# The division of a softmax moved from TensorE transposes to DMA, in six of eight batches

## Chip, cores and metric

One core of a Trainium2 chip runs the whole program. The metric is the device time of one execution in microseconds; the lower, the better.

## What is computed

A transformer block of four parts over x of shape (8, 512, 256), each with a layer norm before it and the input added after it: attention A, a feed-forward net, a retention-like attention B, and the same feed-forward net again. The change lies in attention A alone. Cut to what matters:

```python
att = einsum('bhqd,bhkd->bhqk', q, k) / sqrt(HEAD_DIM)      # 16 heads of 16
att = att + (log_sparse + log(decay + 1e-09))               # depends on distance only
att = softmax(att, axis=-1)
out = einsum('bhqk,bhkd->bhqd', att, v)
out = out + 0.2 * sigmoid(q . mean(k)) * mean(v)
return out.reshape(B, T, 256) @ Wo + bo
```

Softmax needs one division for each row and head. The kernel multiplies the unnormalised probabilities by v first and divides the 16 values of a head by the row's sum afterwards.

## The kernel before

**Tiles and loops.** Batches b (8) times groups g (4 heads each) give 32 items i = 4b + g. An item has eight score steps. In a step TensorE makes a 128x1024 tile of scores `s` for two heads, VectorE takes its row maxima (`mr`), and, ten steps later, TensorE makes the transposed scores `t` of another pair of heads with the maximum already subtracted. ScalarE takes the exponential (`p`), and VectorE or GpSimd multiplies by the table of distances `dec_a`. `pv_item` (line 539) multiplies by v: the tile `pv` is 128x512, 32 rows for each of the four heads, of which 16 are values, one is the row's sum (v carries a column of ones) and the others are unused. All 512 queries stand side by side.

**The division.** `post_units(i)` (line 555) makes up to three units. `evacuate`: ScalarE copies `pv` from PSUM to `num`. `divide`: TensorE turns `num` with four 128x128 transposes, so that queries lie on partitions; VectorE takes the reciprocals of the sums (`rd`, 128x16) and multiplies them into `a_tok`. `turn`, after each second group: TensorE turns half of `a_tok` back with four transposes, and ScalarE copies them into `aT`, where the 128 rows of a half are 8 heads of 16 values. `wo_unit` (line 599) multiplies `aT` by Wo.

**Order.** All engines' instructions are pinned to the order in which the program writes them. That order is planned: a loop at the end keeps an estimated clock for each engine, and work is a chain of `Unit`s (line 292) with a cost on TensorE (`pe`), costs on other engines after it (`then`), predecessors (`after`), things that it gives or needs (`gives`, `needs`), and banks of PSUM. `start_of` (766) says when a unit may start, `issue` (778) writes it and moves the clocks. The loop writes score steps and, between them, units of the other chains: the next batch's projections (`front1`, `front2`), the rest of earlier batches (`rest`: Wo, both feed-forward nets, attention B), and `posts`, the chain of `post_units`, which is looked at first. A unit without TensorE's cost is written as soon as its start is no more than 300 ns ahead of TensorE's planned clock. `turn` of `front2` writes the next batch's `kT` and `qT` by way of DRAM; for keys its step is 32(b - 1) + 14, where the batch's first score is step 32b.

**Queues.** All transfers but the shift of the maxima (`shift`, line 492, on ScalarE's queue) go through `move` (line 90) on SP's queue, in program order. Small PSUM tiles (`misc`, line 210) share three banks. In the profile line 69 is the helper for VectorE, ScalarE and GpSimd, 205 a matmul, 208 a transpose, 91 a transfer of SP.

Of the kernel before, what the change touches and what calls it, by code (L numbers as in the profile page):

```python
# [9 lines left out]
F32 = mybir.dt.float32  # L10
# [5 lines left out]
P = 128  # L16
B, T, D = 8, 512, 256
NH, HD = 16, 16
HH = 8
NG = 4  # L20
NT = T // P
NC = D // P
# [13 lines left out]
def tile_kernel(  # L36
# [37 lines left out]
    dve, act, gps = Engine(nc.vector), Engine(nc.scalar), Engine(nc.gpsimd)  # L74
# [4 lines left out]
    at = ctx.enter_context(tc.tile_pool(name="at", bufs=2))  # L79
    rs = ctx.enter_context(tc.tile_pool(name="rs", bufs=2))  # L80
    dr = ctx.enter_context(tc.tile_pool(name="dr", bufs=1, space=bass.MemoryType.DRAM))
# [8 lines left out]
    def move(to, src):  # L90
        tc.keep_in_program_order(nc.sync.dma_start(to, src))
# [115 lines left out]
    def flip(o, i):  # L207
        tc.keep_in_program_order(nc.tensor.transpose(o, i, ident))  # L208

    def misc(name):  # L210
        return ps_m.tile([P, 512], F32, tag="m", name=name)
# [43 lines left out]
    bb = const.tile([P, 5], F32, tag="bb", name="bb")  # L255
    wr = {}

    def plain(j):
        ps = misc(f"wr{j}")
        for o in range(NC):  # L260
            for c in range(NC):
                flip(ps[:, o * D + c * P : o * D + (c + 1) * P], wqk_in[:, c, j, o * P : (o + 1) * P])
        wr[j] = rs.tile([P, NC, D], F32, tag="xr", bufs=3, name=f"wr{j}")
        act.copy(wr[j].rearrange("p o d -> p (o d)"), ps)

    def product():
# [233 lines left out]
    probs, pv = {}, {}  # L500
# [49 lines left out]
        probs.pop((i, t, 0)), probs.pop((i, t, 1))  # L550


    a_tok, aT = {}, {}

    def post_units(i):
        b, g = divmod(i, NG)
        s = {}

        def evacuate():
            num = at.tile([P, T], F32, tag="num", name=f"num_{i}")  # L560
            act.copy(num, pv[i])
            s["num"] = num

        def divide():
            if g == 0:
                a_tok[b] = at.tile([P, NT, D], F32, tag="atok", bufs=1, name=f"atok_{b}")
                aT[b] = at.tile([P, NC, T], F32, tag="aT", name=f"aT_{b}")
            ps = misc(f"num_{i}")
            for t in range(NT):
                flip(ps[:, t * P : (t + 1) * P], s["num"][:, t * P : (t + 1) * P])  # L570
            pn = ps.rearrange("p (t h d) -> p t h d", h=4, d=32)
            rd = at.tile([P, NT, 4], F32, tag="rd", name=f"rd_{i}")
            dve.reciprocal(rd, pn[:, :, :, HD])
            dve.tensor_tensor(
                a_tok[b][:, :, g * 64 : (g + 1) * 64].rearrange("p t (h d) -> p t h d", d=HD),
                pn[:, :, :, :HD], rd.unsqueeze(3).to_broadcast([P, NT, 4, HD]), ALU.mult,
            )

        def turn():
            c = g // 2  # L580
            ps = misc(f"aT_{i}")
            for t in range(NT):
                flip(ps[:, t * P : (t + 1) * P], a_tok[b][:, t, c * P : (c + 1) * P])
            act.copy(aT[b][:, c, :], ps)

        u = [Unit(evacuate, then=(("ACT", 600),))]
        u.append(Unit(divide, 520, (("DVE", 700),), after=u[-1:]))
        if g % 2:
            u.append(Unit(turn, 520, (("ACT", 600),), after=u[-1:], gives=("aT", b) if g == NG - 1 else None))
        return u  # L590
# [155 lines left out]
    for u in order0[:7]:  # L746
        u.fn()
    late_loads()
    plain(0), plain(1)
    for u in order0[7:10]:  # L750
        u.fn()
# [4 lines left out]
    clock = {"PE": 0, "DVE": 0, "ACT": 0, "POOL": 0}  # L756
# [9 lines left out]
    def start_of(u):  # L766
        if any(x not in given for x in u.needs) or any(a.done is None for a in u.after):
            return None
        if u.takes and held:
            return None  # L770
        t = max([a.done for a in u.after] + [clock["PE"] if u.pe else 0])
        return max(t, banks[u.banks - 1]) if u.banks else t

    def fetch(b):
        xs[b] = load_x(b)
        given.add(("x", b))

    def issue(u):
        t = start_of(u)
        u.fn()  # L780
        if u.pe:
            clock["PE"] = t = t + u.pe
        t += 100
        for e, ns in u.then:
            clock[e] = t = max(clock[e], t) + ns + 60
        u.done = t
        for _ in range(u.banks):
            banks.popleft()
            banks.append(t)
        if u.takes:  # L790
            held.append(u)
        if u.frees:
            held.pop()
        if u.gives:
            given.add(u.gives)
            if u.gives[0] == "wo" and u.gives[1] + 3 < B:
                fetch(u.gives[1] + 3)
# [35 lines left out]
    def step(t):  # L833
# [3 lines left out]
        if n is not None:  # L837
            pv_item(n)
            at_ += 1000
            if n % 8 == 7:  # L840
                us = post_units(n // 8)
                made = Unit(None)
                made.done = at_ + 100
                us[0].after.append(made)
                posts.extend(us)
# [52 lines left out]
    t, credit, share = 0, 0, 0  # L898
    while t < LAST or any(chains) or posts:
        while True:  # L900
            ready = [
                c for c in [posts] + chains
                if c and not c[0].pe and c[0].step <= t and start_of(c[0]) is not None
                and start_of(c[0]) <= clock["PE"] + 300
            ]
            if not ready:
                break
            for c in ready:
                issue(c.pop(0))
# [21 lines left out]
        if take and best is None:  # L931

            c = min((c for c in [posts] + chains if c and start_of(c[0]) is not None), key=lambda c: start_of(c[0]))
            clock["PE"] = max(clock["PE"], start_of(c[0]))
            issue(c.pop(0))
        elif take:
            if best[1] is not posts:
                credit -= best[1][0].pe
            issue(best[1].pop(0))
        else:  # L940
            step(t)
            t += 1
            left = sum(u.pe for c in chains for u in c) - tail_work
            share = max(0, left) / max(1, LAST - t)
            credit = min(credit, share) + share
# [109 lines left out]
```

## Time and profile before

| | |
|---|---|
| median of three runs | 1343.71 us (1343.48 to 1344.67) |
| the profiled execution | 1341.52 us |
| its span, first to last instruction | 1339.7 us |
| TensorE (PE) busy | 1256.3 us, 94% |
| VectorE (DVE) busy | 811.0 us, 61% |
| ScalarE (ACT) busy | 450.0 us, 34% |
| GpSimd (POOL) busy | 405.8 us, 30% |
| transfers through SP's queue | 31.10 MB, 10.1% of the time of 16 DMA engines |

PE is matrix multiplication, PEld the load of its weights, which overlaps it. Matmuls are pipelined, so that a group's drawn lengths overlap what follows. A row of the groups names output and inputs (with buffer numbers left out), their shapes, how many there were, the busy time, the mean of one in ns, and then the idle time of that engine just before, with what ended it. The profile shows one execution; 1.8 us of its time lie outside its span.

### The profile page before, as it was taken

How to read it: one execution, taken by the hardware profiler on the slowest of the kernel's cores; microseconds unless marked ns; L12 is line 12 of the kernel's file. 1: busy time of each engine (PE TensorE's matmuls, PEld its weight loads, DVE VectorE, ACT ScalarE, POOL GpSimd, SP SyncE). 2: the span in 40 equal slices, each digit the busy share in tenths (PEclk: the TensorE clock that was granted, in tenths of full speed). 3: DMA queues.
4: the chain of work that ended last, by engine and by line, in shares of the span. 5: the costliest groups of instructions: out<-in, count | busy, mean ns of one | idle time of the engine just before them, and what ended most of it. 6: DMA issues, size and time to landing. Idle time of an engine off the chain costs nothing. (4 is left out here: it accounts for less than half of the span.)

```text
span 1339.7 us, 15533 instructions
## 1 busy us (share of the span) xinstructions
PE 1256.3 (94%) x6116; PEld 623.3 (47%) x6116; DVE 811.0 (61%) x1323; ACT 450.0 (34%) x646; POOL 405.8 (30%) x461
## 2 busy tenths in 40 slices
PE   6899888999899999999999999999999899999988
PEld 3333232534354455453443554544444445455665
DVE  4588885667656774657856666657755575343130
ACT  2044434333434334433334334333333333321201
POOL 4165542324412432215332323214321232222010
PEclk9599999989899999999999999999999999998999
DMA  5440030012000210004000310003000000000000
GB/s 133 133 80 1 1 80 1 1 26 55 1 17 1 62 19 1 1 17 80 1 1 1 74 22 1 1 9 73 1 1 5 12 1 1 1 17 1 0 16 16
DMA packets 22798, 32.34 MB, mean 24 GB/s; under 512 B 3627, under 2 KB 13228, under 8 KB 22446
## 3 DMA queue, kind: packets, MB, share of 16 engines
q1 hardware_dynamic: 22086, 31.10, 10.1%
q8 instruction: 48, 0.79, 0.3%
q10 hardware_dynamic: 640, 0.26, 0.1%
q14 instruction: 24, 0.20, 0.1%
HBM read 18.50 MB, written 12.58 MB: 23 GB/s over the span
## 5 line engine op out<-in xcount | busy, mean ns | idle before, releaser
L69 DVE TENSOR_REDUCE mr<-s 128x2 f32<-128x1024 f32 x256 | 312.8, 1222 | 251.7 <-PE t L205 237.2
L69 ACT ACTIVATE p<-t 128x1024 f32<-128x1024 f32 (+1 forms) x290 | 263.8, 924 | 519.3 <-PE t L205 476.3
L69 POOL TENSOR_TENSOR p<-p,dec_a 128x512 f32<-128x512 f32 x182 | 233.1, 1301 | 507.6 <-ACT p L69 495.0
L205 PE MATMUL s<-kT,qT 32*128 32x512 f32 x1024 | 295.3, 660 | 49.3 <-DVE mr L69 44.4
L205 PE MATMUL t<-qT,kT 32*128 32x512 f32 x1024 | 294.7, 642 | 0.3 <-ACT p L69 0.3
L69 DVE TENSOR_TENSOR p<-p,dec_a 128x512 f32<-128x512 f32 x330 | 228.9, 735 | 21.0 <-ACT p L69 20.8
L205 PE MATMUL x<-w_sb,h_x 128*128 128x256 f32 x1024 | 233.9, 384 | 0.0
L205 PEld LDWEIGHTS x<-w_sb,h_x 128*128 128x128 f32 x1024 | 190.8, 190 | 54.5 <-issue 30.1
L205 PEld LDWEIGHTS s<-kT,qT 32*128 32x128 f32 x1024 | 81.2, 189 | 221.8 <-DVE mr L69 97.5
L205 PE MATMUL pv<-p,va 128*32 128x512 f32 x1024 | 151.7, 612 | 2.9 <-DVE p L69 2.4
L69 ACT ACTIVATE h_x<-hx,vec 128x512 f32<-128x512 f32 x128 | 88.0, 687 | 151.8 <-PE hx L205 151.8
L205 PE MATMUL hx<-xT_f,w_sb 128*128 128x512 f32 x256 | 120.2, 609 | 0.7 <-ACT xT_f L69 0.7
L205 PE MATMUL hx<-xT_g,w_sb 128*128 128x512 f32 x256 | 119.3, 609 | 0.7 <-ACT xT_g L69 0.7
L69 DVE TENSOR_TENSOR x<-x,x 128x256 f32<-128x256 f32 x64 | 27.1, 423 | 148.3 <-PE x L205 148.3
L205 PEld LDWEIGHTS t<-qT,kT 32*128 32x128 f32 x1024 | 80.5, 184 | 15.9 <-ACT p L69 7.8
L205 PEld LDWEIGHTS hx<-xT_g,w_sb 128*128 128x128 f32 x256 | 46.8, 193 | 63.5 <-issue 58.1
L205 PEld LDWEIGHTS hx<-xT_f,w_sb 128*128 128x128 f32 x256 | 46.5, 194 | 58.3 <-issue 51.6
L205 PEld LDWEIGHTS pv<-p,va 128*32 128x32 f32 x1024 | 23.3, 108 | 79.3 <-issue 37.0
L69 POOL TENSOR_TENSOR x<-x,row 128x256 f32<-128x256 f32 x64 | 48.0, 770 | 32.1 <-DVE xn_f L69 21.4
L69 POOL TENSOR_TENSOR rc<-rc,rs 128x512 f32<-128x512 f32 x32 | 42.3, 1342 | 5.6 <-DVE rs L69 5.6
L205 PE MATMUL bs<-xT_r,ret 128*128 128x512 f32 (+3 forms) x128 | 38.0, 442 | 0.0
L205 PE MATMUL bo<-ret 128*128 128x256 f32 x160 | 36.6, 383 | 0.0
(130 smaller groups left out, 1020.1 us busy)
## 6 DMA issues: line engine op xcount, KB each, us to landing
dk<-rc SPq DMA_DIRECT2D x16, 256.0 KB, 2.9
kT<-dk SPq DMA_DIRECT2D x32, 128.0 KB, 3.2
dq<-rc SPq DMA_DIRECT2D x16, 256.0 KB, 2.9
qT<-dq SPq DMA_DIRECT2D x32, 128.0 KB, 3.8
out_dram<-x SPq DMA_DIRECT2D x32, 128.0 KB, 1.7
x<-in_x_dram SPq DMA_DIRECT2D x7, 512.0 KB, 3.6
w_sb<-in_w_dram SPq DMA_DIRECT2D x2, 1024.0 KB, 10.1
x<-in_x_dram SPq DMA_DIRECT2D x2, 256.0 KB
```

The source lines that it names most:

```text
L69: ins = f(*a, **k)
L205: tc.keep_in_program_order(nc.tensor.matmul(o, lhsT=l, rhs=r, start=start, stop=stop))
```

## The change

For batches 1 to 6 `post_units` hands over to a new function. `evacuate` copies `pv` to `num` as before, and then sends the four rows of sums (512 numbers each) to 128 partitions with 16 columns (`sums`), and each head's 16 rows of values straight to their rows of `aT`: five transfers a group. After each second group `invert` takes the reciprocals of 128x32 sums on VectorE, stores them in DRAM (`d_rec`) and loads them back so that each of the eight rows is repeated on 16 partitions (`rec`). `divide` multiplies that half of `aT` by `rec` on VectorE. Batches 0 and 7 keep the old way. The planner gets times for the transfers (4500 and 5800 ns) that no engine's clock is charged for. The transposed Wq and Wk of attention B (`wr`), which are used at the start alone, move into the memory of `x1`, for space.

```diff
+    wr_both = rs.tile([P, NT, D], F32, tag="x1", bufs=1, name="wr")
...
-        wr[j] = rs.tile([P, NC, D], F32, tag="xr", bufs=3, name=f"wr{j}")
+        wr[j] = wr_both[:, 2 * j : 2 * j + 2, :]
...
+    d_rec = [dr.tile([2, 4, T], F32, tag=f"d_rec{i}", name=f"d_rec{i}") for i in range(2)]
+
+    def post_units_dma(i):
+        b, g = divmod(i, NG)
+        c = g // 2
+
+        def evacuate():
+            num = at.tile([P, T], F32, tag="num", name=f"num_{i}")
+            act.copy(num, pv[i])
+            if g == 0:
+                aT[b] = at.tile([P, NC, T], F32, tag="aT", name=f"aT_{b}")
+            if g % 2 == 0:
+                sums[c] = at.tile([P, 2, HD], F32, tag="sums", name=f"sums_{b}_{c}")
+            move(sums[c][:, g % 2, :], num[HD:P:32])
+            for h in range(4):
+                at_row = (g % 2) * 64 + h * HD
+                move(aT[b][at_row : at_row + HD, c, :], num[h * 32 : h * 32 + HD])
+
+        def invert():
+            d = d_rec[c]
+            dve.reciprocal(sums[c], sums[c])
+            move(d.rearrange("g h (x y) -> (h x) g y", y=HD), sums[c])
+            sums["rows", c] = at.tile([P, T], F32, tag="rec", name=f"rec_{b}_{c}")
+            move(
+                sums["rows", c],
+                d.rearrange("g h t -> (g h) t").unsqueeze(1).to_broadcast([8, HD, T]),
+            )
+
+        def divide():
+            dve.tensor_mul(aT[b][:, c, :], aT[b][:, c, :], sums["rows", c])
+
+        u = [Unit(evacuate, then=(("ACT", 600), (None, 4500)))]
+        if g % 2:
+            u.append(Unit(invert, then=(("DVE", 350), (None, 5800)), after=u[-1:]))
+            u.append(Unit(divide, then=(("DVE", 700),), after=u[-1:], gives=("aT", b) if g == NG - 1 else None))
+        return u
+
     def post_units(i):
         b, g = divmod(i, NG)
+        if 0 < b < B - 1:
+            return post_units_dma(i)
...
         for e, ns in u.then:
-            clock[e] = t = max(clock[e], t) + ns + 60
+            if e is None:
+                t += ns
+            else:
+                clock[e] = t = max(clock[e], t) + ns + 60
```

More of the change, by code (lines that the diff above doesn't have):

```diff
@@ L550, in pv_item @@
         probs.pop((i, t, 0)), probs.pop((i, t, 1))
-    a_tok, aT = {}, {}
+    a_tok, aT, sums = {}, {}, {}
+    d_rec = [dr.tile([2, 4, T], F32, tag=f"d_rec{i}", name=f"d_rec{i}") for i in range(2)]
[29 more added lines that the diff above has]
+        return u
     def post_units(i):
         b, g = divmod(i, NG)
+        if 0 < b < B - 1:
+            return post_units_dma(i)
         s = {}
```

## The prediction

> **What bounds the kernel now.** I read the windows by stage first, then the groups, then the waits of TensorE, then its timeline around the steps that go. The windows (length, then busy time and count of PE, PEld, DVE, ACT and POOL, then clock, DMA share, GB/s):
>
> ```profile
> 0.00:70.00 70.00, 53.28 (x193) 24.34 (x193) 37.99 (x63) 12.40 (x30) 22.07 (x41) 0.80 0.50 127
> 170.00:330.00 160.00, 144.99 (x757) 66.64 (x753) 110.62 (x180) 55.67 (x76) 51.62 (x58) 0.98 0.16 34
> 650.00:810.00 160.00, 158.84 (x810) 80.22 (x810) 105.31 (x178) 56.72 (x77) 47.55 (x54) 1.00 0.09 21
> 970.00:1130.00 160.00, 152.31 (x771) 74.83 (x770) 97.08 (x153) 59.83 (x78) 41.73 (x46) 1.00 0.01 4
> ```
>
> The reader is to see that TensorE is without work for only 15.0, 1.2 and 7.7 us of three 160 us stages, while VectorE is busy about two thirds and the DMA engines stand nearly empty. The kernel is bound by TensorE's queue nearly everywhere. The changed batches lie in these stages. The groups (busy us, mean ns, then idle just before and its releaser):
>
> ```profile
> L69 DVE TENSOR_REDUCE mr<-s 128x2 f32<-128x1024 f32 x256 | 312.8, 1222 | 251.7 <-PE t L205 237.2 <-PE s L205 13.4
> L69 DVE TENSOR_TENSOR p<-p,dec_a 128x512 f32<-128x512 f32 x330 | 228.9, 735 | 21.0 <-ACT p L69 20.8
> L208 PE MATMUL num<-ident,num 128*128 128x128 f32 x128 | 20.1, 280 | 0.2 <-ACT num L69 0.2
> L69 DVE TENSOR_TENSOR atok<-num,rd 128x256 f32<-128x256 f32 x32 | 13.6, 425 | 1.1
> L208 PE MATMUL aT<-ident,atok 128*128 128x128 f32 x64 | 10.2, 281 | 0.6 <-DVE atok L69 0.6
> L69 ACT COPY aT<-aT 128x512 f32<-128x512 f32 x16 | 9.3, 583 | 16.6 <-PE aT L208 16.6
> L69 DVE RECIPROCAL rd<-num 128x16 f32<-128x16 f32 x32 | 8.0, 249 | 7.3 <-PE num L208 7.2
> ```
>
> The four groups on `num`, `atok` and `rd` and the two on `aT` are the division and the turn that six batches lose. The waits of TensorE itself (us, times, longest):
>
> ```profile
> PE s L205 <- DVE mr L69: 44.4, 43, 2.4
> ...
> PE wo L205 <- ACT aT L69: 1.2, 3, 0.7
> ```
>
> In 43 of 256 score steps TensorE waits for VectorE's maxima; in the other direction VectorE waits for TensorE before 148 of the 256 maxima, 237.2 us or 1.6 us each. So VectorE has some slack, but not everywhere. The timeline of TensorE (start, length, count of merged instructions):
>
> ```profile
> 521.12 0.60 PE L208 MATMUL num<-ident,num 128*128 128x128 f32 x4
> 521.65 0.70 PE L205 MATMUL s<-kT,qT 32*128 32x512 f32 x2
> ...
> 522.72 0.66 PE L208 MATMUL aT<-ident,atok 128*128 128x128 f32 x4
> 523.21 1.03 PE L205 MATMUL x<-w_sb,h_x 128*128 128x256 f32 x4
> ```
>
> Four transposes are drawn 0.60 and 0.66 us long, but the next instruction starts 0.53 and 0.49 us after them. That interval, not the drawn length, is what leaves the queue.
>
> **What the skill says.** The Trainium skill, "Perfetto Trace Analysis", section "Identifying the Most-Contended Engine", says that matmul busy share is a poor measure[...]; the trace agrees (0.60 drawn, 0.53 in the queue), so I price by start-to-start. "DMA: Bandwidth & Descriptors", section "Issuing engines are not separate DMA queues", says that all queues share 16 engines and that an issuer pays only its sequencer's time; here four `kT<-dk` issues take 1.74 us of SP, 0.43 each. The same page, section "Why a DMA increments its semaphore by 16 and not by 1", says that the split over engines follows the slowest dimension of both sides: for four rows of sums that is likely 4 engines, not 16. No run here shows how long such a transfer takes to land. "VectorE: DVE Perf Modes", section "Why `tensor_tensor` can't do 2×_2P or 4×", leaves the new multiplication at one element a cycle; the trace has 735 ns for this shape.
>
> **The change, part by part.** Six batches have 24 groups and 12 pairs of groups.
>
> *Transposes removed from TensorE.* 24 of `num` and 12 of `aT`, four each: 36 slots of 0.50 us (between 0.44 and 0.53 in the places I looked at) make 18.0 us. All of them stand in TensorE's queue in stages where it is 91 to 99% busy, so I count them whole.
>
> *Waits of TensorE removed.* `wo` for the copy of `aT` 1.2 us, `aT` for `atok` 0.6, `num` for its copy 0.2: 2.0 us over eight batches, and what is left in two batches is little. Each is small because the planner puts other units between. I count 2.0 us as the upper end and as the value.
>
> *VectorE.* Removed: 24 x (0.249 + 0.425) = 16.2 us. Added: 12 reciprocals of 128x32, about 0.3 us each (the 128x16 one takes 0.249), and 12 multiplications at 0.735: 12.4 us. Net 3.8 us less; hidden by TensorE, worth nothing by itself.
>
> *ScalarE and PSUM.* 12 copies of 0.583 = 7.0 us go; ScalarE is 34% busy, so nothing. 36 times a bank of the three small ones is no longer held. Of TensorE's 83 us idle 44.4 are waits for maxima and 16.7 lie in the first 70 us; of the other 22 a quarter, 5 us, may be late banks. I count nothing, and those 5 us as a gain for one rival.
>
> *SP's queue.* Each group adds one sums and four value transfers, each pair a store and a broadcast load: 24 x 5 + 12 x 2 = 144 issues at 0.43 to 0.55 us, 62 to 79 us spread over some 900. SP stands waiting for hundreds of microseconds now, so its own time is hidden. But SP takes its queue in order: the store waits for the reciprocal, the load for the store's landing, and the next batch's `dk`/`kT` writes, the stores of `out` and a load of `x` stand behind. `kT` is wanted 18 score steps after it is due (256 steps lie between 38.0 and 1156.2 us, 4.4 us each, so 79 us), so 5 us there are hidden; if that cover were gone, the first score of each batch would pay them, 6 x 5 = 30 us. ScalarE's shift transfers share completion semaphores with SP's, eight transfers apart; those have landed long before, nothing.
>
> *New waits on VectorE.* Behind the waiting reciprocal or multiplication stand the maxima and the masks; TensorE waits for them. The reciprocal needs the sums' issue and landing: 0.43 + 2.9 (the row `dk<-rc`) = 3.3 us; ends 0.43 + 1.7 (`out_dram<-x`) and 0.43 + 5.1 (the longest `kT` landing), also for the 4 engines. The code sets it 4.5 us after the copy, so it is covered; at the upper end it is 1.0 short. The multiplication needs reciprocal, issue, landing, issue, landing: 0.3 + 0.5 + 2.9 + 0.5 + 3.2 = 7.4 us, ends 5.8 and 11.5. The code sets it about 6.2 us later, and VectorE often comes later than TensorE's clock (the reciprocal `rd` at 261.3 us follows transposes of 257.50). I take a shortage of 0.5 us, ends 0 and 5.3. 12 x 0.5 = 6 us on VectorE; the slack of 1.6 us takes most of it, and about a quarter (43 of 256 steps have none, others little) reaches TensorE: 1.5 us.
>
> *Later `aT`.* `wo` of a batch starts some 10 us later; other batches' units fill the queue. Batch 7 keeps the old way, so the end does not change. `wr` moving into `x1`'s memory costs nothing: it is read long before `x1` is written.
>
> Sum: -18.0 - 2.0 + 1.5 = -18.5 us. The profiled execution took 1341.52 us (span 1339.7 and 1.8 around it), giving 1323.0; the median shown is 2.19 above it, so 1343.71 - 18.5 = 1325.2 us.
>
> **The rivals.**
> *The freed slots become waits.* Where transposes stood between two score steps they covered VectorE's 1.22 us maximum; without them TensorE waits for `mr`. For it: 44.4 us of such waits today. Against: 1.2 us idle in a whole stage shows that the planner finds other work. If half the slots are lost: 1343.71 - 9 = 1334.7 us.
> *More than the slots.* The freed banks also let units start earlier: 5 us more, and no stall: 1343.71 - 18.0 - 2.0 - 5 = 1318.7 us.
> *Slower: VectorE held by DMA.* If 64-byte pieces land slowly, all 24 waits on VectorE run long. It decides when the mean wait goes above the slack of 1.6 us by 20 / 24 = 0.8 us, at 2.4 us. At the upper ends VectorE stands 12 x 1.0 + 12 x 5.3 = 76 us; less 24 x 1.6 = 38 of slack, 38 reach TensorE: 1343.71 - 20 + 38 = 1361.7 us. For it: no row of before shows such a transfer. Against: due times with 4.5 and 5.8 us in them.
> *No change.* A gain and a stall of the same size: 1343.7 us.
>
> **How the numbers follow.** Forecast, 1320 to 1331: 0.58. Half the slots, 1331 to 1341: 0.18. More, below 1320: 0.09. No change: 0.05. Slower: 0.10. A difference under 0.2% (2.7 us) can't be told from none. So faster 0.58 + 0.18 + 0.09 = 0.85, same 0.05, slower 0.10. Beyond 1339 lie 0.17 and below 1318 some 0.04, so the range is 1318 to 1339.
>
> **What would show it.** Right: `num` with 32 and `aT` with 16 transposes left; TensorE's busy time about 20 us lower and its idle time (83 us) about as now; "PE s <- DVE mr" near 44 us; VectorE's waits for transfers under 10 us in all. Wrong: those at 40 us or more, with `mr` waits up by as much; landings of the sums or the store above 5 us; or TensorE's idle time up by the time that the transposes left.

## The result, and the profile after

The changed kernel takes 1328.61 us (median of four, 1326.82 to 1330.21) against 1344.19 (1343.48 to 1344.97) for the kernel before: a ratio of 0.9884, 95% interval 0.9867 to 0.9901, or 15.6 us less. The forecast was 18.5 us less. The profiled executions are 13.5 us apart, 1341.52 and 1328.06.

The windows of the kernel after, columns as in those of before:

```profile
...
170.00:330.00 160.00, 141.05 (x744) 64.80 (x742) 115.78 (x188) 56.53 (x77) 57.79 (x66) 0.99 0.18 40
...
650.00:810.00 160.00, 157.06 (x777) 78.21 (x776) 106.85 (x177) 57.43 (x78) 54.31 (x63) 1.00 0.12 28
...
sum 1326.00, PE 1237.71 PEld 608.15 DVE 799.18 ACT 443.71 POOL 409.11; mean PE 112.52 PEld 55.29 DVE 72.65 ACT 40.34 POOL 37.19
```

TensorE is busy 1237.7 us, 18.6 less than before, as the forecast said ("about 20"). But its idle time, span less busy, went from 83.4 to 88.5 us. A window has a fixed length, so a shorter stage does not show in it: in the first one TensorE does less work in 160 us than before (744 matmuls instead of 757) and is idle for 19.0 us instead of 15.0.

Another difference stands beside the work. The profile gives the mean clock that TensorE was granted, as a share of its full clock: 0.978 before and 0.982 after. Of 98 executions of the kernel before in the later sets, 40 had a clock of 0.976 and took 1344.1 us on average, and 13 had 0.981 and took 1338.6. Four executions of the changed kernel, of nine, had 0.980 and took 1329.8. So at nearly the same clock the change is worth some 9 us; the rest, of 15.6 us here and of 12.6 when the changed kernel was run again, goes with a higher clock. The busy time divides in the same way: busy time times clock, an estimate of the work at full clock, is 1228.7 us before and 1215.4 after, so some 13 of the 18.6 us are less work. Why the changed kernel has the higher clock is not shown.

The products with v (`pv`) mark where the time went. Their first and last start, before and after:

```profile
L205 PE MATMUL pv<-p,va x1024: 588/616/1063, 70.8 to 1195.3; 128*32 128x512 f32 x171
L205 PE MATMUL pv<-p,va x1024: 588/616/1063, 69.2 to 1185.3; 128*32 128x512 f32 x171
```

Up to the first start the changed kernel is 1.6 us ahead, where only the place of `wr` differs. From the first to the last it takes 1116.1 us instead of 1124.5, which is 8.4 less at a mean clock of 0.99 in both. From the last to the end it takes 140.9 us instead of 144.4, which is 3.5 less, although no transpose was removed there: TensorE has 482 matmuls to do in both, at a clock of 0.96 instead of 0.95.

The groups of the kernel after:

```profile
L69 DVE TENSOR_REDUCE mr<-s 128x2 f32<-128x1024 f32 x256 | 312.7, 1222 | 263.6 <-PE t L205 249.7 <-PE s L205 12.5
L69 DVE TENSOR_TENSOR aT<-aT,rec 128x512 f32<-128x512 f32 x12 | 8.5, 710 | 0.0
L208 PE MATMUL num<-ident,num 128*128 128x128 f32 x32 | 5.3, 287 | 0.8 <-ACT num L69 0.8
L69 DVE RECIPROCAL sums<-sums 128x32 f32<-128x32 f32 x12 | 4.1, 342 | 0.0
L69 DVE TENSOR_TENSOR atok<-num,rd 128x256 f32<-128x256 f32 x8 | 3.4, 425 | 0.3
L208 PE MATMUL aT<-ident,atok 128*128 128x128 f32 x16 | 2.6, 287 | 0.8 <-DVE atok L69 0.8
```

The transposes fell to 32 of `num` and 16 of `aT`. The two new operations of VectorE have an idle time of 0.0 before them: in all of this execution VectorE never waited for a transfer. The waits of TensorE after (us, times, longest):

```profile
PE s L205 <- DVE mr L69: 46.2, 55, 2.0
PE pv L205 <- DVE p L69: 6.2, 8, 2.5
...
PE wo L205 <- DVE aT L69: 0.9, 1, 0.9
...
PE aT L208 <- DVE atok L69: 0.8, 1, 0.8
PE num L208 <- ACT num L69: 0.8, 1, 0.8
```

The waits for maxima are 1.8 us more, those of `pv` for a mask 3.8 more (2.4 before). The timeline of SP's queue and of VectorE for the first pair of batch 1 shows why the transfers are covered:

```profile
212.80 0.59 SPq L91 DMA_DIRECT2D sums<-num  x1
213.45 2.43 SPq L91 DMA_DIRECT2D aT<-num  x4
216.00 0.51 SPq L91 DMA_DIRECT2D d_rec<-sums  x1
217.71 0.66 SPq L91 DMA_DIRECT2D rec<-d_rec  x1
```

```profile
213.83 1.23 DVE L69 TENSOR_REDUCE mr<-s 128x2 f32<-128x1024 f32 x1
214.97 0.34 DVE L69 RECIPROCAL sums<-sums 128x32 f32<-128x32 f32 x1
223.04 1.23 DVE L69 TENSOR_REDUCE mr<-s 128x2 f32<-128x1024 f32 x1 [7.73 <-PE t L205]
224.19 1.28 DVE L69 TENSOR_TENSOR p<-p,dec_a 128x512 f32<-128x512 f32 x2
225.39 0.69 DVE L69 TENSOR_TENSOR aT<-aT,rec 128x512 f32<-128x512 f32 x1
```

The sums have landed when VectorE is done with the next maximum, and `rec`, asked for at 217.71, is used 7.7 us later, after work that stands ahead of it anyhow.

### The profile page after: what moved, and what is told of

It is laid out like the page before. It is cut to its first block, busy times and chain, and to the rows that moved or that the text cites. A ratio compares the mean times of both kernels' runs of the same rounds, so it can differ in the third digit from the quotient of the medians.

```text
span 1326.2 us, 15505 instructions
## 1 busy us (share of the span) xinstructions
PE 1237.7 (93%) x5972; PEld 608.2 (46%) x5972; DVE 799.2 (60%) x1299; ACT 443.7 (33%) x634; POOL 409.1 (31%) x461
## 5 line engine op out<-in xcount | busy, mean ns | idle before, releaser
L205 PE MATMUL s<-kT,qT 32*128 32x512 f32 x1024 | 293.7, 657 | 51.2 <-DVE mr L69 46.2
```

The costliest lines, as they stand in the source:

```text
L205: tc.keep_in_program_order(nc.tensor.matmul(o, lhsT=l, rhs=r, start=start, stop=stop))
```

## The experiments

Single executions of one kernel were further apart in the later sets (those of before from 1335.46 to 1345.63 us), so the ratios to before, with their intervals, are what to compare; 0.001 is 1.3 us.

**The division left out.** Batches 1 to 6 keep only the transfers of values; sums, reciprocals, the trip to DRAM and the multiplication are left out, so `aT` is not divided there. TensorE's order is that of the changed kernel, in the trace too.

```diff
-            move(sums[c][:, g % 2, :], num[HD:P:32])
...
-            u.append(Unit(invert, then=(("DVE", 350), (None, 5800)), after=u[-1:]))
+            u.append(Unit(lambda: None, then=(("DVE", 350), (None, 5800)), after=u[-1:]))
```

> The changed kernel without the division in batches 1 to 6: no sums, reciprocals, trip to DRAM or multiplication, only the four transfers of values per group; planned order as in the changed kernel. Theory (queue slots, transfers hidden): within 2 us of the changed kernel, 1326.6 to 1328.6 us. Rival (transfers: the 3 us between forecast and result were lost to VectorE and SP held by the division's transfers): 1323 to 1326 us. In both, the 12.4 us of VectorE that go too count little.

1328.61 us, ratio 0.9890 (0.9873 to 0.9907); the changed kernel has 0.9884, and 0.9902 when run again. Nothing is gained by leaving the division out. In its profile TensorE's wait for maxima is the same as in the changed kernel:

```profile
PE s L205 <- DVE mr L69: 45.9, 55, 2.0
PE pv L205 <- DVE p L69: 6.8, 9, 2.5
```

So the sums' transfers, the DRAM trip and 12.6 us of VectorE cost nothing that can be measured, and the 3 us by which the forecast was too high are not there.

**The lead taken away.** Reciprocal and multiplication written right behind the second group's transfers, with the planner's clocks and the written order of TensorE unchanged. (In the trace two score matmuls start ahead of two waiting ones in nine places; else the order is the same.)

```diff
                 move(aT[b][at_row : at_row + HD, c, :], num[h * 32 : h * 32 + HD])
+            if g % 2:
+                invert()
+                divide()
```

> The changed kernel with reciprocal and multiplication written right after the second group's transfers, so that VectorE waits for the transfers in full; TensorE's order as in the changed kernel. It prices the waits that the planned lead hides. Theory: VectorE waits some 2.5 us for the sums and 4 to 5 us for store and load, 12 times, 80 to 90 us in all; less slack of 1.6 us at 24 places, 40 to 50 us reach TensorE: 1370 to 1380 us. Rival (the lead does not matter, transfers land within VectorE's slack): under 1335 us.

1419.3 us, ratio 1.057 (1.0548 to 1.0591): 90 us slower than the changed kernel. The waits of VectorE in this kernel:

```profile
DVE aT L69 <- DMA rec<-d_rec: 80.6, 12, 7.4
...
DVE sums L69 <- DMA sums<-num: 18.2, 12, 2.4
```

VectorE waits 98.8 us for transfers, and the program is 90 us longer. The stall does not arrive whole, though. TensorE's idle time is 137.1 us instead of 88.5 (span 1418.8 less busy 1281.7): 48.6 us more, within the 40 to 50 that the theory let through. Its other half is what the theory had no term for: TensorE's busy time is 44.0 us longer for the same 5972 matmuls, with a mean granted clock of 0.948 instead of 0.982. Busy time times clock is 1215.0 us here and 1215.4 in the changed kernel, so by this estimate the lower clock accounts for all of the 44. The theory had the direction, and nearly the waits (80 to 90 us), but not the total (1370 to 1380).

**The slots put back.** The changed kernel with blocks of four idle transposes of constants on TensorE, read by nobody: 36 blocks in the first kernel, 72 in the second. Apart from the blocks, TensorE, VectorE, ScalarE and GpSimd run in the order of the changed kernel, in the traces too.

```diff
+            for n in range(1 + g % 2):              # second kernel: range(2 * (1 + g % 2))
+                ps = misc(f"back_{i}_{n}")
+                for t in range(NT):
+                    flip(ps[:, t * P : (t + 1) * P], wo_sb[:, t // 2, (t % 2) * P : (t % 2 + 1) * P])
```

> The changed kernel with 36 idle blocks of four transposes put back on TensorE, one after each copy of pv to num and two after each second one, of constant data, read by nobody; all else and all orders as in the changed kernel. Theory (queue slots: the gain is 36 slots of 0.50 us): the whole gain is given back, 1328.6 + 18 = 1346.6 us, and TensorE's idle time stays near 88 us. Rival (waits: part of the slots only covered waits for the maxima): 1335 to 1339 us, with TensorE's idle time some 8 to 10 us lower. Second rival (the gain came from freed small PSUM banks and freed VectorE or ScalarE time): these blocks use banks too, but nothing of VectorE or ScalarE, so under 1335 us.

> The changed kernel with 72 idle blocks of four transposes, twice as many as were removed, in the places of the first flips run. It prices the second 36. Theory (first 36 partly covered waits for the maxima, the second set does not): the second set costs 18 us, more than the first: 1357 to 1361 us. Rival (every slot costs the same): twice the first set's 13 us, 1353 to 1356 us.

36 blocks: 1341.5 us, ratio 0.9992 (0.998 to 1.0005). 72 blocks: 1354.82 us, ratio 1.0089 (1.0064 to 1.0115). From the changed kernel (0.9884, and 0.9902 when run again) to 36 blocks is 0.0090 to 0.0108, or 12 to 14.5 us, and from 36 to 72 is 0.0097, or 13 us. The first and last start of `pv` in the two profiles:

```profile
L205 PE MATMUL pv<-p,va x1024: 589/616/1063, 74.4 to 1203.8; 128*32 128x512 f32 x171
L205 PE MATMUL pv<-p,va x1024: 589/616/1062, 70.2 to 1212.9; 128*32 128x512 f32 x171
```

Between them lie 1129.4 and 1142.7 us, where the changed kernel has 1116.1: 13.3 us for each 36 blocks, at a mean clock of 0.99 in all three. So each block costs 0.37 us at the end, while a single one takes 0.49 us of the queue, as before:

```profile
191.36 0.66 PE L208 MATMUL back<-ident,wo_sb 128*128 128x128 f32 x4
191.85 1.03 PE L205 MATMUL wo<-wo_sb,aT 128*128 128x256 f32 x4
```

The queue slots are most of the gain: put back alone, they take nearly all of it away. None of the expected ranges for 36 blocks was met: the theory in its strict form (0.50 each, 1346.6 us) is too high, its rival (1335 to 1339) too low, and the second rival (under 1335, the gain from banks, VectorE and ScalarE) fell. The idea that only the first set covers waits fell too: the second set costs the same. A block also holds one of the three small banks, so this is the price of slot and bank together.

The kernel with 72 blocks was profiled at a clock of 0.981, close to the changed kernel's 0.982. Its TensorE is busy 32.0 us longer (1269.7), 0.44 for each block, and idle 5.4 us less (83.1), 0.07 for each block. So of the 0.13 us that 0.37 lacks to 0.50 about half is waits that a block fills, and the other half is busy time that it does not add. The waits for maxima fall from 46.2 us over 42.5 to 40.9. The profiled execution of 36 blocks took 1345.42 us, 17.4 more than the changed kernel's, but at a clock of 0.978.

**Later `aT` alone.** The kernel before with all its transposes, where in batches 1 to 6 the planner gives `aT` 9 us after the copy. No instruction is added, and the planner may move its clock on where a score step can't start.

```diff
-            u.append(Unit(turn, 520, (("ACT", 600),), after=u[-1:], gives=("aT", b) if g == NG - 1 else None))
+            late_by = ((None, 9000),) if 0 < b < B - 1 else ()
+            u.append(Unit(turn, 520, (("ACT", 600),) + late_by, after=u[-1:]))
+            u.append(Unit(lambda: None, after=u[-1:], gives=("aT", b) if g == NG - 1 else None))
```

> The kernel before, old division and all its transposes kept, with one part of the change alone: in batches 1 to 6 the planner lets Wo's units start 9 us later than the copy to aT, about as much later as the new way makes them. No instruction is added or removed; the order of units between score steps moves. Theory (later aT and the new order give back some of the slots' gain): 1345 to 1352 us. Rival (later aT is hidden, as forecast): 1341 to 1344 us.

1348.07 us, ratio 1.0044 (1.0025 to 1.0062): 5.9 us slower than before, as the theory expected. The clock makes this too small: six of its eight executions had 0.981 and took 1348.6 us on average, 10 us more than before at 0.981. The wait for maxima in its profile:

```profile
PE s L205 <- DVE mr L69: 50.8, 55, 3.7
```

It was 44.4 us in 43 waits before and is 50.8 in 55 now; the changed kernel has 55 as well. Nothing but the order of the units moved. From the first `pv` to the last it takes 1131.5 us, 7.0 more than before, and from there to the end 144.0, nearly as before (144.4). A reading that no run isolates: when Wo's units come later, more score steps follow each other without enough between them.

**Leads twice as long, and shorter.** The changed kernel with 9000 and 11600 ns instead of 4500 and 5800, and with 2500 instead of 4500 (there the planner may move its clock on, too).

> The changed kernel planned with leads of 9000 and 11600 ns for the transfers, twice as long. Theory (no transfer waits on VectorE in the changed kernel; what the new order of units costs or gives is chance): within 4 us of the changed kernel, on either side, 1325 to 1332 us. Rival (hidden waits on the transfers cost part of the gain): 3 us faster or more, 1325 us or less.

> The changed kernel with 2500 instead of 4500 ns as the lead for the first transfers (the reciprocal was seen to start 2.0 us after the copy where nothing kept it). Theory (later aT costs through the order): aT comes 2 us earlier, so a little faster, 1325 to 1329 us, with waits of VectorE for transfers under 5 us in all. Rival (the lead was needed): VectorE waits 10 us or more in all, and 1333 us or more.

Twice as long: 1346.53 us, ratio 1.0032 (1.0021 to 1.0043). That is 17 us slower than the changed kernel and eats the whole gain; both the theory (4 us of chance) and its rival failed. TensorE is idle for 99.3 us in its profile, 10.8 more than in the changed kernel, and its wait for maxima is the largest of all runs:

```profile
PE s L205 <- DVE mr L69: 56.2, 56, 2.1
```

Shorter: 1334.43 us, ratio 0.9927 (0.99 to 0.9953), which is 3 to 6 us slower than the changed kernel where "a little faster" was expected. No wait of VectorE for a transfer stands in its profile, so the rival's cause is not it either. The loss goes with the clock: its five executions at 0.974 to 0.977 took 1332.1 to 1335.6 us, and the sixth, at 0.985, took 1325.2, less than any of the changed kernel. Its TensorE is busy 1246.1 us in the profile, 8.4 more than in the changed kernel, but times the clock of 0.974 that is 1213.7, where the changed kernel has 1215.4. Why the clock is lower is open.

**An order's chance, and the memory of `wr`.** The kernel before with 540 in place of 520 ns as the planned cost of these transposes, and the kernel before with `wr` in `x1`'s memory.

> The kernel before with 540 instead of 520 ns as the planner's cost of the transposes of num and aT: no instruction is added or taken away, only the order of some units moves. Theory (an order's chance is worth a few microseconds): 1340 to 1348 us, not exactly the time of before. Rival (orders are worth nothing): within 1 us of before.

> The kernel before with one part of the change alone: the transposed Wq and Wk of attention B in the memory of x1. Theory: nothing, 1343 to 1345 us. Rival (placement in memory or the start matters): 2 us or more away from 1344.2, in the direction of the change.

1341.45 us, ratio 0.9988 (0.9978 to 0.9999), and 1343.1 us, ratio 0.9994 (0.9982 to 1.0006). A small shift of the order was worth 1.6 us, and `wr` nothing that can be measured.

**The new way in more batches.** In all eight, and in batches 0 to 6; the planner may move on where a score step can't start.

```diff
-        if 0 < b < B - 1:
+        if b < B - 1:                               # all eight: if True
...
-            if not take and s_step is None:
-                raise AssertionError("nothing to do")
+            take = take or s_step is None
```

> The changed kernel with the new way in all eight batches (and a planner that may move its clock on to the next unit where a step can't start). Theory (queue slots): 12 more slots of 0.40 to 0.50 us go, 5 to 6 us less than the changed kernel, if the longer way to aT of the last batch is filled by the rest of batch 6: 1323 us. Rival (the last batch's way to aT, some 6 us longer, ends uncovered): the gain is eaten, 1328 to 1330 us.

> The changed kernel with the new way in batch 0 too (batches 0 to 6; the planner may move its clock on where a step can't start). It splits the loss of the version with all eight. Theory (in batch 0 nothing else is there to fill the longer way to aT; the last batch pays at its end): about half of the loss each, 1336 to 1342 us. Rival (the loss is at the end alone): 1326 to 1329 us.

All eight: 1352.7 us, ratio 1.0065 (1.0044 to 1.0086). Seven: 1341.23 us, ratio 0.9994 (0.9982 to 1.0007). So fewer transposes made it slower than the changed kernel, by some 12 us for batch 0 and 9 more for batch 7 (by difference). With batch 7 the end, from the last `pv` on, grows from 140.9 to 153.3 us. SP's queue in the kernel with seven, at the end of batch 0:

```profile
164.07 0.59 SPq L91 DMA_DIRECT2D sums<-num  x1
164.70 2.41 SPq L91 DMA_DIRECT2D aT<-num  x4
172.60 2.24 SPq L91 DMA_DIRECT2D dk<-rc  x2
177.28 1.74 SPq L91 DMA_DIRECT2D kT<-dk  x4
179.12 0.38 SPq L91 DMA_DIRECT2D d_rec<-sums  x1
183.59 0.67 SPq L91 DMA_DIRECT2D rec<-d_rec  x1
```

The next batch's keys (`dk`, `kT`) came first in the program. SP waits for them and for their landing, and the reciprocals, ready at 173.04 + 0.34, are stored only at 179.12. The multiplication follows at 187.62, and TensorE waits:

```profile
PE wo L205 <- DVE aT L69: 9.4, 2, 8.5
```

That is 8.5 us in one place, where batch 0 has no earlier batch whose units could fill it. It is not the whole loss: this profile is of the fastest of 14 executions (1334.39 us), with TensorE idle for 94.4 us, 5.9 more than in the changed kernel. It had a clock of 0.979, the other 13 had 0.966 to 0.975, and the rest of the 12 us goes with that. All eight batches had 0.958 to 0.973. Whether these waits lower the clock or something else does is not shown.

**The changed kernel again**, beside the leads and the eight batches:

> The changed kernel once more, beside the variants of this set on one chip. All theories: a ratio to before of 0.988, within its interval of 0.9867 to 0.9901.

1329.74 us, ratio 0.9902 (0.9885 to 0.9919). None of the versions tried beats it.

## Why the prediction was right, and what it mis-sized

The main cause was right, and the closeness of 18.5 and 15.6 is in part luck: the slots brought less than forecast, lateness took more, and two gains that the prediction did not name made up for it.

*Transposes removed, 36 x 0.50 = 18.0 us.* The mechanism is shown: the idle blocks give 13.3 us per 36 back at the same clock, with nothing else changed. The queue interval was right (0.49 measured again), but not all of it reaches the end. "I count them whole" was the step, some 5 us too high. The rival "the freed slots become waits" was right in kind: a quarter of the slots' time did not arrive, where it said half, and about half of that quarter was waits.

*Waits removed, 2.0 us.* Of the three rows that were to go only the wait of `wo` for ScalarE's copy shrank, to 0.2 us. `aT` for `atok` and `num` for its copy, which stay in two batches, are 0.8 each, and `wo` waits 0.9 for VectorE's multiplication: 2.7 us in all. Idle time is up by 5.1 us in the profiles. It was no term to add.

*VectorE, ScalarE, banks, SP's own time: nothing.* Leaving the division out, with 12.6 us of VectorE, changed nothing; ScalarE's copies and the banks were not taken apart. VectorE's busy time fell by 11.8 us where 3.8 were worked out; the multiplication and reciprocal took 710 and 342 ns (735 and 300 used), so the rest lies in other groups. (The prediction speaks of four groups on `num`, `atok` and `rd`; its lines show three.)

*New waits, 1.5 us.* None showed. The kernel without lead shows the parts: `sums` landed some 1.9 us after its issue began (3.3 used), and from the reciprocal's start to the multiplication's was 6.9 us (7.4 used). The price behind them was too low, but not by its slack: of 98.8 us of stall, 48.6 became idle time of TensorE, less than the 60 that 1.6 us of slack at each of 24 places would leave. What had no term is the 44.0 us of longer busy time at a lower clock. The planned leads kept the slower rival away.

*Later `aT`: "other batches' units fill the queue", 0 us.* This step failed. Lateness alone costs 5.9 us in the kernel before, and 10 at the same clock, beside more waits for maxima; leads twice as long cost 17. The changed kernel shows the same sign: from the first to the last `pv` the slots should have brought 13.3 us, and 8.4 came (11.3 in the second run, at a clock of 1.00), so 2 to 5 us were lost there in other ways. From the kernel before with late `aT` (1.0044) to the changed one (0.9884 and 0.9902) is 0.0142 to 0.0160, or 19 to 21 us; 13.3 of that are the slots, 3 lie after the last `pv`, and the orders of these two kernels are not the same, so the remainder is not taken apart.

*The end: not in the prediction but for "the end does not change".* From the last `pv` on the changed kernel takes 3.5 us less. This is not the chance of one execution: the changed kernel, its second run, the one without the division and the two with blocks have 139.8 to 141.0 us there, and before, `wr` alone, the 540 ns and late `aT` have 144.0 to 144.6. With the shorter lead it is 144.5 again, though its transposes are gone as well. So it comes with the order that the planner happened to make, and a part of it is the clock.

*The clock: not in the prediction.* Busy time "about 20 us lower" came out at 18.6, but by the estimate above some 13 of it are work and the rest is the higher clock.

## What to carry to other kernels

Where an engine's queue is full, work taken off it was worth less than its start-to-start interval here (0.37 of 0.49 us); putting it back as idle work, in an unchanged order, measures that price. Work moved to DMA is free only while its landing is planned for: with the lead it cost nothing, without it 90 us for 98.8 us of stall, half of that as longer matmuls at a lower clock. A result that comes later had a price here, 6 to 10 us, even if nobody waits for it, as the order of the other work changes with it; where there was no other work, as in the first batch, the wait stood open. And before a difference of 1% is put down to work, compare the clocks: in the kernel before, 0.976 and 0.981 were 5.5 us apart.

## What the runs showed of the hardware that was not expected

- Stalls cost twice. In the kernel without lead TensorE's idle time rose by 48.6 us and its busy time by 44.0, at a clock of 0.948 instead of 0.982. The Trainium skill, "TensorE: Matmul & The Clock Gate", section "Part 1: The HAM clock gate (the "warmup" mystery)", says that the array's clock follows how busy it has lately been. These numbers agree with it (1281.7 x 0.948 = 1215.0 and 1237.7 x 0.982 = 1215.4 us), but no run here isolates a single stall.
- Issuing took SP 0.60 us for `sums`, 0.66 for `rec` and 0.38 for most of `d_rec`, where 0.43 to 0.55 was used; one group's five transfers held SP from 212.80 to 215.88 us, longer than the sums took to land (1.9).
- A transfer of 512-element rows in 64-byte pieces (`sums`, 8 KB) landed in about 1.9 us from the start of its issue (217.10 to 219.00 in the kernel without lead), less than the 2.9 of the 256 KB row that stood in for it.
